# Attention over a 0/1 adjacency: more heads' sums from 0/1 patterns, and where the patterns are made

## The chip, the cores and the metric

The kernel runs on one core of a Trainium2 chip. The time is the device time of one execution in microseconds (us). TensorE (PE) multiplies matrices, VectorE (DVE), ScalarE (ACT) and GpSimd (POOL) work on vectors, SyncE (SP) only issues DMAs; ACT and POOL issue DMAs too.

## What is computed

Four graph layers follow one another on x (2708 x 512, float32) with one adjacency adj (2708 x 2708, 0/1, symmetric, with ones on its diagonal). Each is x + layer(relu(layernorm(x)), adj). Layers 0, 1 and 3 are a normalised sum, a mean of the first 64 neighbours and a mean of all neighbours, each with dense products. Layer 2 is the attention, which the change is about:

```python
Wh = jnp.einsum('nd,hdo->hno', x, W)              # 8 heads, 64 outputs each
f1 = jnp.einsum('hno,ho->hn', Wh, a1)
f2 = jnp.einsum('hno,ho->hn', Wh, a2)
e = jax.nn.leaky_relu(f1[:, :, None] + f2[:, None, :], negative_slope=0.2)
e = jnp.where(adj[None, :, :] > 0, e, NEG_INF)
attention = jax.nn.softmax(e, axis=-1)
h_prime = jnp.einsum('hnm,hmo->hno', attention, Wh)
out = jax.nn.elu(h_prime)
```

## The kernel before

**Tiles and steps.** The 2708 nodes lie in NC = 22 chunks of R = 126 rows (the last has 62). The attention works through units: u0 and u1 are head 0's output columns 0 to 1384 and 1384 to 2708, u2 to u7 the heads 1 to 6 whole, u8 and u9 head 7's two column parts. Each unit runs over the 22 chunks m of neighbours; a step is one pair of unit and chunk, 220 in all. In the step the kernel does this:

- `make` (L883, DVE) builds the weights t of the chunk, 126 rows by the unit's columns: max(row value, column value) times the 0/1 adjacency vT (uint8, kept in SBUF). The exponentials of leaky_relu factor into a row part `rb` and a column part `ec`, so that the maximum of the two is the weight. There are TILES = 4 buffers of t.
- `scale` (ACT) multiplies the chunk's rows of Wh by the factor `ef` into whs (L872), and, unless the step is "by side", a column of ones too (L874). There are 4 buffers of whs and 3 of wh, loaded by SP three chunks at a time.
- `multiply` (PE, in the helper at L1066) adds Wh-weighted rows into the accumulators av, in float32, and, unless by side, the weights' sums from t into the accumulators sums.
- A step *by side* gets its sums otherwise. `compare` (ACT, L901) turns t into a bf16 0/1 pattern b (2 buffers) by a very steep Sigmoid, which tells which of the two factors was the maximum; `multiply_sides` (PE, one step later) multiplies it by `parts`, three bf16 pieces that add up to each float32 factor. `by_side` holds for chunks with m % 5 in (1, 3, 4), 13 of 22, in the heads 1 to 6.

**Sums by side need a count.** The patterns give the sums over the neighbours on one side. The rest comes from the sum over all neighbours of the second factor: for each by-side chunk, `mask` (L1138, ACT) copies the chunk's adjacency as bf16 into four buffers of tag "x" (126 x 677 each), and `count_neighbors` (PE, L1150) multiplies it by `parts2`, the pieces for the heads, into two accumulators adj_sums; after the last one, eight copies (L1163) send them out. The masks are planned for the steps from 11 on, chunk i's count for step 13 + 2i: five counts stand in u0, eight in u1.

**split** (L1122 to L1127) makes the pieces: ACT casts a piece (L1122), DVE subtracts it (L1124), three rounds for each of two factors; the last ACT copy (L1127) fills parts2.

**Head changes.** The next head's row values are loaded by `load_row1` (SP, 126 copies of a row, 1332.8 KB, two buffers rb) and raised by `exp_row` (ACT, L847). Exp and Sigmoid need different function tables, so each exp_row in a by-side stretch brings two table loads. `evict` copies a finished unit's accumulators (ACT, L1105) and stores them.

**What sets the order.** The main loop hands out each step's operations in the order scale, make (three steps ahead), compare (one ahead), multiply, multiply_sides (one behind), then what `behind(s, fn, ...)` has put into `plan` for that step. A scheduler then orders each engine's queue by priority and estimated times, so that a planned step isn't a fixed place; `tc.issue_after(ins)` keeps an operation behind a named one. Buffers that are reused add waits. PE, ACT, DVE, POOL and SP each work through their own queue in order.

The layer-3 loads `load3` are planned for the last 16 steps and take "x" buffers (5). The rows a1 and a2 of the dense stage ahead (`arow`) have buffers of their own, and the bias row b3, which L1258 adds in layer 3, has one too.

Of the kernel before, what the change touches and what calls it, by code (L numbers as in the profile page):

```python
# [8 lines left out]
F32 = mybir.dt.float32  # L9
F32R = mybir.dt.float32r  # L10
BF16 = mybir.dt.bfloat16
# [3 lines left out]
AF = mybir.ActivationFunctionType  # L15
# [5 lines left out]
P = 128  # L21

R = 126
# [7 lines left out]
SLOPE2 = 0.2  # L31
# [13 lines left out]
def fast_layers(  # L45
# [36 lines left out]
    nc = tc.nc  # L82
    N, D = x_in.shape
    H, _, O = w2.shape
    NC = -(-N // R)
    NF = D // P
# [5 lines left out]
    def rows(c):  # L92
        return min(R, N - c * R)
# [17 lines left out]
    XBUFS = 5  # L111
# [8 lines left out]
    weights = ctx.enter_context(tc.tile_pool(name="weights", bufs=2))  # L120
    dram = ctx.enter_context(tc.tile_pool(name="dram", bufs=1, space=DRAM))

    common = ctx.enter_context(tc.tile_pool(name="common", bufs=2))

    ps = ctx.enter_context(tc.tile_pool(name="ps", bufs=8, space=PSUM, reuse_waits="tile"))
# [47 lines left out]
            nc.sync.dma_start(w[:, i], src[i * P : (i + 1) * P, :])  # L173
        return w

    def load_row(pool, src, name, tag=None):

        t = pool.tile([P, D], F32, name=name, tag=tag or name)
        nc.sync.dma_start(t, bass.AP(tensor=src.tensor, offset=src.offset, ap=[[0, P], [1, D]]))
        return t  # L180

# [165 lines left out]
    vT = []  # L347
# [69 lines left out]
    with ExitStack() as ring_ctx:  # L417
        ring = ring_ctx.enter_context(tc.tile_pool(name="ring", bufs=NC - 1, side="right"))
# [29 lines left out]
        with tc.tile_pool(name="l0", bufs=2) as wk:  # L448
            units = [(g, m) for g in range(len(groups)) for m in range(NC)]
            tiles, uppers, acc, sums, xs = {}, {}, {}, {}, {}  # L450
# [344 lines left out]
    BY_SIDE = [m for m in range(NC) if m % 5 in (1, 3, 4)]  # L795
# [6 lines left out]
    cut = EARLY * R // 8 * 8  # L802
    units = [(h, 0, N) for h in range(H)]
# [3 lines left out]
    steps = [(u, m) for u in range(len(units)) for m in range(NC)]  # L807

    def by_side(u, m):
        return 0 < units[u][0] < H - 1 and m in BY_SIDE  # L810

    whd = dram.tile([N, D], F32, name="whd")
    avT = dram.tile([D, N], F32, name="avT")
# [2 lines left out]
    sumT = dram.tile([NS, N], F32, name="sumT")  # L816
# [4 lines left out]
    at = at_ctx.enter_context(tc.tile_pool(name="att", bufs=1, reuse_waits="tile"))  # L821
# [3 lines left out]
    parts = at.tile([R, NC * H * 8 + S], BF16, name="parts")  # L825
    nc.gpsimd.memset(parts, 0.0)
    parts_of = parts[:, : NC * H * 8].rearrange("p (m h k) -> p m h k", h=H, k=8)
    parts2 = at.tile([R, NC, H, 3], BF16, name="parts2")
    nc.gpsimd.memset(parts2, 0.0)
    one6 = at.tile([R, S], F32, name="one6")  # L830
    nc.gpsimd.memset(one6, 0.0)
    nc.gpsimd.memset(one6[:, 6:7], 1.0)
    row, weight, wh, whs, acc, sides, made = {}, {}, {}, {}, {}, {}, []

    def load_row1(h, lo, hi):

# [7 lines left out]

    def exp_row(h, lo, hi):
        t = row[h][:, lo:hi]
        nc.scalar.activation(t, t, AF.Exp, scale=1.0 - SLOPE2)  # L847


    GROUP = 3  # L850
# [15 lines left out]
    def scale(s):  # L866

        u, m = steps[s]
        h, q = units[u][0], rows(m)
        t = at.tile([R, O + S], F32, name="whs", bufs=4)  # L870
        by = ef[:q, m, h : h + 1]
        nc.scalar.activation(t[:q, :O], wh.pop((u, m))[:q], AF.Copy, scale=by)  # L872
        if not by_side(u, m):
            nc.scalar.activation(t[:q, O:], one6[:q], AF.Copy, scale=by)  # L874
        whs[s] = t

    def make(s):
        u, m = steps[s]
        h, lo, hi = units[u]
        q = rows(m)  # L880
        g, k = where[m]
        t = at.tile([R, N], F32, name="t2", bufs=TILES)
        ins = nc.vector.scalar_tensor_tensor(  # L883
            t[:q, : hi - lo],
            row[h][:q, lo:hi],
            ec[:q, m, h : h + 1],
            vT[g][:q, k, lo:hi],
            op0=ALU.max,
            op1=ALU.mult,
        )  # L890
        weight[s] = t
        made.append(ins.ins)
# [16 lines left out]

    l2p = ctx.enter_context(ExitStack())  # L910
    pp = l2p.enter_context(tc.tile_pool(name="l2p", bufs=2, side="right", reuse_waits="tile"))
    ar = [load_row(pp, a, f"arow{i}") for i, a in enumerate((a1, a2))]

    products, firsts = {}, {}

# [73 lines left out]
    e3_ctx = ctx.enter_context(ExitStack())  # L989
    e3 = e3_ctx.enter_context(tc.tile_pool(name="e3", bufs=2, side="right", reuse_waits="tile"))  # L990
    er = e3.tile([R, NC, H], F32, name="er", bufs=1)
    rest = e3.tile([R, NC, H], F32, name="rest", bufs=1)
    kept3, l3_weights = {}, []


# [56 lines left out]
    def pieces(w):  # L1052

        k = -(-w // 512)
        cuts = [round(i * w / k) for i in range(k + 1)]
        return list(zip(cuts, cuts[1:]))

    def sizes_of(u):
        _, lo, hi = units[u]
        return (hi - lo) // 2, (hi - lo) // 4  # L1060
# [38 lines left out]
    def evict(u, which):  # L1099
        h, lo, hi = units[u]  # L1100
        size = sizes_of(u)[which]
        dst, height, step = (sumT, 7, S) if which else (avT, O, O)
        for p, (a, b) in zip(acc[u][which], pieces(size)):
            t = common.tile([P, D], F32, name="out", tag="t", bufs=3)
            nc.scalar.copy(t[:, : b - a], p[:, : b - a])  # L1105
            for j in range(P // step):
                nc.sync.dma_start(
                    dst[h * height : (h + 1) * height, lo + j * size + a : lo + j * size + b],
                    t[j * step : j * step + height, : b - a],
                )  # L1110

    def split():

        nc.scalar.mul(eb, ec, -STEEP * ABOVE)
        for i in range(2):
            e = ef
            if i:
                nc.vector.tensor_tensor(rest, ec, ef, ALU.mult)
                e = rest
            for k in range(3):  # L1120
                part = parts_of[:, :, :, 3 * i + k]
                nc.scalar.copy(part, e)  # L1122
                if k < 2:
                    nc.vector.tensor_tensor(rest, e, part, ALU.subtract)  # L1124
                    e = rest
        heads = slice(1, H - 1)
        nc.scalar.copy(parts2[:, :, heads], parts_of[:, :, heads, 3:6])  # L1127


    quarter = N // 4  # L1130
    counted, masks = [], {}

    def mask(i, j):
        m = BY_SIDE[i]
        q = rows(m)
        g, k = where[m]
        t = masks[i, j] = common.tile([P, D], F32, name="x", bufs=XBUFS).bitcast(BF16)
        nc.scalar.copy(t[:q, :quarter], vT[g][:q, k, j * quarter : (j + 1) * quarter])  # L1138

    def count_neighbors(i):  # L1140
        m = BY_SIDE[i]
        q = rows(m)
        if i == 0:
            counted.extend(
                ps.tile([P, 512], F32, name="adj_sums", tag="ps") for _ in pieces(quarter)
            )
        w = parts2[:q, m].rearrange("p h k -> p (h k)")
        for p, (a, b) in zip(counted, pieces(quarter)):
            for j in range(4):
                nc.tensor.matmul(  # L1150
                    p[j * S : j * S + 3 * H, : b - a],
                    w,
                    masks[i, j][:q, a:b],
                    start=(i == 0),
                    stop=(i == len(BY_SIDE) - 1),
                )
        if i < len(BY_SIDE) - 1:
            return
        for p, (a, b) in zip(counted, pieces(quarter)):
            t = common.tile([P, D], F32, name="out", tag="t", bufs=3)  # L1160
            for j in range(4):
                own = slice(j * S, j * S + 3 * H)
                nc.scalar.copy(t[own, : b - a], p[own, : b - a])  # L1163
                nc.sync.dma_start(
                    sumT[7 * H :, j * quarter + a : j * quarter + b], t[own, : b - a]
                )

    def exp_nodes():
# [10 lines left out]
    def behind(s, fn, *args):  # L1179
        plan.setdefault(s, []).append((fn, args))  # L1180
# [3 lines left out]
    behind(4, exps2, slice(EARLY, NC))  # L1184
    behind(5, load_row1, *units[1])
    behind(6, exp_row, *units[1])
    behind(9, split)
    behind(30, load_l3_weights)
    behind(30, exp_nodes)
    for u in range(2, len(units)):  # L1190
        if units[u][1] == 0:
            s = max(1, u - 1) * NC
            behind(s + 4, load_row1, units[u][0], 0, N)
            behind(s + 8, exp_row, units[u][0], 0, N)
    for u in range(len(units)):
        behind((u + 1) * NC - 1, evict, u, 0)
        behind(min((u + 1) * NC, len(steps) - 1), evict, u, 1)
    for i in range(len(BY_SIDE)):
        for j in range(4):
            behind(11 + 2 * i + j // 2, mask, i, j)  # L1200
        behind(13 + 2 * i, count_neighbors, i)

    for at_step, fn, c in (
        (16, load3, 0),
# [33 lines left out]

    with ExitStack() as stack:
        ring = stack.enter_context(tc.tile_pool(name="ring3", bufs=NC - 1, reuse_waits="tile"))  # L1240
        b3 = e3.tile([P, D], F32, name="b3", bufs=1)
        nc.sync.dma_start(
            b3, bass.AP(tensor=bias3.tensor, offset=bias3.offset, ap=[[0, P], [1, D]])
        )
# [688 lines left out]
def kernel(tc: tile.TileContext, *args: bass.AP):  # L1933

    nc = tc.nc
    with tc.tile_pool(name="verdict", bufs=1) as pool:
        verdict = pool.tile([1, 1], I32, name="verdict")
        fast_layers(tc, *args, verdict)
        odd = nc.values_load(verdict[0:1, 0:1], min_val=0, max_val=P + 1)
        with tc.If(odd > 0):  # L1940
            general_layers(tc, *args)
# [32 lines left out]
```

## Time and profile before

| what | us |
|---|---|
| median of three runs (1822.24 to 1826.04) | 1825.34 |
| the profiled execution | 1825.62 |
| its span | 1823.8 |
| attention, first to last matmul of L1066 | 856.6 to 1417.1 |
| PE's first matmul of u0, u1, u2 | 856.6, 898.6, 938.3 |
| PE's first matmul of u3, u4, u5, u6, u7 | 1002.4, 1073.8, 1138.5, 1203.4, 1268.3 |
| PE's first matmul of u8, u9 | 1334.9, 1374.1 |
| DVE's first make of u0, u1, u2 | 833.5, 892.8, 933.3 |
| DVE's first make of u7, u8, u9 | 1261.0, 1327.6, 1368.9 |
| L1138, a mask copy of 126 x 677 on ACT, 48 of them (and 4 of 62 rows) | 0.76 |
| L1105, a copy of an accumulator on ACT | 0.43 to 0.53 |

A line of groups names the source line, the engine, the operation, output and inputs with their shapes, how many there were, their busy time and the mean in ns of one; after the last bar stands how long the engine sat idle just before them, and what it then waited for. A line of waits adds these up by waiter and releaser. A table of stretches gives, for each stretch of the span, its length and the busy time of each engine. Matmuls overlap one another, so the time from one's start to the next one's is shorter than the mean of one.

### The profile page before, as it was taken

Reading aid. Unit: us, or ns where it says so; the run is one execution under the profiler, and the core shown is the slowest. Engines: PE = TensorE matmul, PEld = TensorE weight load, DVE = VectorE, ACT = ScalarE, POOL = GpSimd, SP = SyncE. Lnnn points to the kernel's source line nnn. Section 1 sums busy time; section 2 is a strip of 40 time slices with the busy share of each in tenths; the row PEclk is TensorE's granted clock in tenths of the full one; section 3 lists DMA queues with packets and bytes.
Section 4 is the critical chain, followed back from the end, with each engine's and each line's share of the span. In section 5 each row is a group of like instructions: output and inputs, shape, how many; then the busy total and the mean of one; then the engine's idle time right before and its main releaser. Section 6 shows DMA issues by size and latency. Waiting matters only on the chain.

```text
span 1823.8 us, 30715 instructions
## 1 busy us (share of the span) xinstructions
PE 1785.4 (98%) x11884; PEld 1041.1 (57%) x11884; DVE 1308.3 (72%) x1836; ACT 796.6 (44%) x1542; POOL 245.2 (13%) x241
## 2 busy tenths in 40 slices
PE   9999999999999999999999999999999999999998
PEld 4456777654448887644544344334444445488776
DVE  4942998855446655788999999999989777533334
ACT  2632777731210000156896676776744566400000
POOL 0101323301110211266000000000000222100000
PEclk9999999999999999999999999999999999999999
DMA  7632666635462211353231121121012444313221
GB/s 247 193 112 67 204 209 199 193 80 115 116 143 58 71 57 46 94 149 104 73 89 35 33 61 41 29 61 53 15 36 53 130 139 131 95 34 109 82 68 45
DMA packets 165553, 176.62 MB, mean 97 GB/s; under 512 B 94830, under 2 KB 115792, under 8 KB 164516
## 3 DMA queue, kind: packets, MB, share of 16 engines
q1 hardware_dynamic: 143170, 131.47, 26.3%
q10 hardware_dynamic: 18484, 33.28, 5.3%
q0 software_dynamic: 3744, 9.82, 1.6%
q8 instruction: 95, 1.56, 0.4%
q14 instruction: 60, 0.49, 0.1%
HBM read 111.35 MB, written 55.15 MB: 91 GB/s over the span
## 4 chain that ended last, share of the span: by engine, by line
PE 77%; DVE 11%; DMA 5%; issue 4%; POOL 1%; ACT 1%; SPq 0%; ACTq 0%; DVEq 0%; POOLq 0%
PE acc L368 32%; PE av L1066 16%; PE nb_ps L184 6%; PE sums L1066 6%; DVE t L883 5%; PE self_ps L184 4%; PE wh_ps L184 3%; PE line_ps L184 2%; PE h_ps L184 2%; DVE cum L494 2%; PE fused_ps L312 2%; PE hT_ps L212 1%; DMA x<-x 1%; DMA rb<-rT 1%; DMA packed<-two 1%
## 5 line engine op out<-in xcount | busy, mean ns | idle before, releaser
L883 DVE SCALAR_TENSOR_TENSOR t<-rb,ec,vT 126x2708 f32<-126x2708 f32 (+2 forms) x220 | 532.4, 2469 | 20.6 <-PE sums L1066 10.9
L368 PE MATMUL acc<-halves,kt 126*126 126x512 f32 x1848 | 435.5, 395 | 3.7 <-DVE kt L741 2.1
L1066 PE MATMUL av<-t,whs 126*32 126x451 f32 (+3 forms) x4576 | 436.5, 515 | 0.6 <-DVE ln_mv L191 0.6
L368 PEld LDWEIGHTS acc<-halves,kt 126*126 126x126 f32 x1848 | 342.6, 186 | 93.1 <-DVE kt L741 6.5
L1066 PEld LDWEIGHTS av<-t,whs 126*32 126x32 f32 (+1 forms) x4576 | 160.2, 110 | 206.9 <-issue 181.7
L368 PE MATMUL acc<-halves,ar 126*126 126x512 f32 x924 | 235.4, 408 | 4.3 <-ACT ar L488 2.4
L901 ACT ACTIVATE b<-t,eb 126x2708 bf16<-126x2708 f32 (+1 forms) x78 | 199.0, 2551 | 21.2 <-DVE t L883 21.0
L368 PEld LDWEIGHTS acc<-halves,ar 126*126 126x126 f32 x924 | 171.0, 189 | 55.4 <-issue 8.1
L193 ACT ACTIVATE ln_rs<-ln_mv,eps 126x1 f32<-126x1 f32 x88 | 25.6, 293 | 341.1 <-DMA x<-x 199.2
L741 DVE SCALAR_TENSOR_TENSOR kt<-lastr,index,vT 126x504 fp32r<-126x504 int16 (+3 forms) x154 | 110.4, 728 | 80.9 <-PE acc L368 80.7
L1291 DVE CAST kt<-vT 126x504 fp32r<-126x504 uint8 (+3 forms) x154 | 55.9, 365 | 138.2 <-PE acc L368 138.2
L1066 PE MATMUL sums<-t,whs 126*32 126x338 f32 (+5 forms) x1568 | 140.5, 451 | 5.1 <-ACT out L1105 5.1
L872 ACT ACTIVATE whs<-wh,ef 126x64 f32<-126x64 f32 x220 | 76.6, 350 | 130.1 <-PE sums L1066 73.7
L1033 POOL TENSOR_SCALAR z<-y 126x512 f32<-126x512 f32 x22 | 44.0, 2000 | 664.8 <-DVE y L1026 656.0
L494 DVE TENSOR_TENSOR_SCAN cum<-ai,deg 126x504 int16<-126x504 int32 (+2 forms) x110 | 128.4, 1180 | 0.6 <-DMA ai<-in_adj 0.6
L522 ACT ACTIVATE cum<-cum,limit 126x504 int16<-126x504 int16 (+3 forms) x132 | 88.1, 667 | 59.9 <-DVE deg L502 58.9
L1066 PEld LDWEIGHTS sums<-t,whs 126*32 126x32 f32 (+1 forms) x1568 | 55.3, 109 | 73.1 <-issue 40.7
L189 DVE BATCH_NORM_STATS2 ln_st<-x 126x6 f32<-126x512 f32 x88 | 60.2, 685 | 45.7 <-DMA x<-x 30.8
L184 PE MATMUL h_ps<-w0s,hT 128*126 128x512 f32 x176 | 81.2, 605 | 4.7 <-ACT hT L214 3.5
L184 PE MATMUL nb_ps<-wfn,hT 128*126 128x512 f32 x176 | 80.7, 602 | 3.1 <-ACT hT L214 3.1
L184 PE MATMUL wh_ps<-w2s,hT 128*126 128x512 f32 (+1 forms) x176 | 79.4, 593 | 0.0
L184 PE MATMUL nb_ps<-wn,hT 128*126 128x512 f32 x176 | 79.2, 592 | 0.0
(182 smaller groups left out, 1870.6 us busy)
## 6 DMA issues: line engine op xcount, KB each, us to landing
x<-x SPq DMA_DIRECT2D x105, 252.0 KB
x<-x ACTq DMA_DIRECT2D x84, 252.0 KB
ai<-in_adj SPq DMA_DIRECT2D x84, 249.0 KB
x<-in_x SPq DMA_DIRECT2D x42, 252.0 KB
rb<-rT SPq DMA_DIRECT2D x7, 1332.8 KB
wh<-whd SPq DMA_DIRECT2D x70, 94.5 KB
packed<-two POOLq DMA_DIRECT2D x44, 124.5 KB, 4.5
whd<-wh SPq DMA_DIRECT2D x21, 252.0 KB
```

The lines of the kernel that those rows point to most:

```text
L184: nc.tensor.matmul(po[:n], lhsT[:, f, :n], w[:, f, :], start=(f == 0), stop=(f == NF - 1))
L189: nc.vector.bn_stats(st[:n], xc[:n])
L368: nc.tensor.matmul(acc[:R], weight[:, k * R : (k + 1) * R], parts[:, i, :], start=(m == 0 and i == 0), stop=(m == NC - 1),)
L494: nc.vector.tensor_tensor_scan(cum[:n, :gw], ai[:n, :gw], ai[:n, :gw], 0.0 if g == 0 else deg[:n, m : m + 1], op0=ALU.add, op1=ALU.max,)
L522: nc.scalar.activation(cum[:n, :gw], cum[:n, :gw], AF.Sign, bias=limit[:n], scale=-1.0, accum_out=signs[:n, m, g : g + 1],)
L741: nc.vector.scalar_tensor_tensor(by_chunk(kt, cs), lastr[:, cs[0] * R : (cs[-1] + 1) * R].rearrange("p (c r) -> p c r", r=R), index[:R, m ...
L872: nc.scalar.activation(t[:q, :O], wh.pop((u, m))[:q], AF.Copy, scale=by)
L883: ins = nc.vector.scalar_tensor_tensor(t[:q, : hi - lo], row[h][:q, lo:hi], ec[:q, m, h : h + 1], vT[g][:q, k, lo:hi], op0=ALU.max, op1=AL ...
L901: nc.scalar.activation(b[:q, : hi - lo], weight[s][:q, : hi - lo], AF.Sigmoid, bias=eb[:q, m, h : h + 1], scale=STEEP,)
L1033: nc.gpsimd.tensor_scalar(z, y, 0.0, None, op0=ALU.min)
L1066: nc.tensor.matmul(p[j * S : (j + 1) * S, : b - a], lhsT, rhs[:, part * size + a : part * size + b], start=(s % NC == 0), stop=(s % NC == ...
L1291: nc.vector.tensor_copy(by_chunk(kt, cs), pattern(m, cs))
```

## The change

- `by_side` holds for u1 to u8: the second part of head 0 and the first part of head 7 are by side too.
- `parts2` covers the 13 by-side chunks only, in two versions by column half: the left half for the heads 1 to 7, the right half for the heads 0 to 6. Six small ACT copies fill it instead of one.
- `mask` is one DMA a chunk, issued by POOL, that reads 126 x 2708 uint8 from vT and writes bf16 into one of the two buffers b of the patterns, instead of four ACT copies into "x" buffers. It is planned for step 6 + i, and the count for step 10 + i. Twelve counts then stand in u0 in the built order, the thirteenth in u1's first step. The counts' column quarters are cut at [0, 692, 1384, 2046, 2708], so that pieces have 346 or 331 columns. In POOL's queue the first two mask DMAs stand ahead of the dense stage's first product, the other eleven each behind a wait on PE, for the count that frees the buffer.
- `load_row1` is planned two steps after the head's start (before: four) and `exp_row` nine (before: eight), and exp_row is kept behind the last scale handed out until then.
- Buffers: the a1 and a2 rows go into a weight buffer ("w"), `rest` into a "t" buffer, the av copies of full heads into "x" buffers, b3 into the ring of layer 3.

```diff
     def by_side(u, m):
-        return 0 < units[u][0] < H - 1 and m in BY_SIDE
+        return 0 < u < len(units) - 1 and m in BY_SIDE
...
-    parts2 = at.tile([R, NC, H, 3], BF16, name="parts2")
+    parts2 = at.tile([R, len(BY_SIDE), 2, H, 3], BF16, name="parts2")
...
     def exp_row(h, lo, hi):
         t = row[h][:, lo:hi]
-        nc.scalar.activation(t, t, AF.Exp, scale=1.0 - SLOPE2)
+        with tc.issue_after(scaled[-1]) if scaled else ExitStack():
+            nc.scalar.activation(t, t, AF.Exp, scale=1.0 - SLOPE2)
...
-    ar = [load_row(pp, a, f"arow{i}") for i, a in enumerate((a1, a2))]
+    arows = weights.tile([P, NF, D], F32, name="arows", tag="w")
+    ar = [load_row(None, a, None, into=arows[:, i]) for i, a in enumerate((a1, a2))]
...
-            t = common.tile([P, D], F32, name="out", tag="t", bufs=3)
+            tag, bufs = ("x", XBUFS) if (lo, hi) == (0, N) and which == 0 else ("t", 3)
+            t = common.tile([P, D], F32, name="out", tag=tag, bufs=bufs)
...
-        heads = slice(1, H - 1)
-        nc.scalar.copy(parts2[:, :, heads], parts_of[:, :, heads, 3:6])
-    quarter = N // 4
+        for i, heads in enumerate((slice(1, H), slice(0, H - 1))):
+            for r in sorted({m % 5 for m in BY_SIDE}):
+                ms = [m for m in BY_SIDE if m % 5 == r]
+                src = parts_of[:, r :: 5, heads, 3:6]
+                at_i = [BY_SIDE.index(m) for m in ms]
+                nc.scalar.copy(parts2[:, at_i[0] : at_i[-1] + 1 : 3, i, heads], src)
+    fourths = [0, cut // 2, cut, (cut + N) // 2, N]
...
-    def mask(i, j):
+    def mask(i):
...
-        t = masks[i, j] = common.tile([P, D], F32, name="x", bufs=XBUFS).bitcast(BF16)
-        nc.scalar.copy(t[:q, :quarter], vT[g][:q, k, j * quarter : (j + 1) * quarter])
+        t = masks[i] = at.tile([R, N], BF16, name="b", bufs=2)
+        nc.gpsimd.dma_start(t[:q], vT[g][:q, k, :N])
...
-            behind(s + 4, load_row1, units[u][0], 0, N)
-            behind(s + 8, exp_row, units[u][0], 0, N)
+            behind(s + 2, load_row1, units[u][0], 0, N)
+            behind(s + 9, exp_row, units[u][0], 0, N)
...
-        for j in range(4):
-            behind(11 + 2 * i + j // 2, mask, i, j)
-        behind(13 + 2 * i, count_neighbors, i)
+        behind(6 + i, mask, i)
+        behind(10 + i, count_neighbors, i)
...
-        b3 = e3.tile([P, D], F32, name="b3", bufs=1)
+        b3 = ring.tile([P, D], F32, name="b3", bufs=1)
```

More of the change, by code (lines that the diff above doesn't have):

```diff
@@ L174, in load_weight, with load_row @@
         return w
-    def load_row(pool, src, name, tag=None):
-        t = pool.tile([P, D], F32, name=name, tag=tag or name)
+    def load_row(pool, src, name, into=None):
+        t = into
+        if t is None:
+            t = pool.tile([P, D], F32, name=name)
         nc.sync.dma_start(t, bass.AP(tensor=src.tensor, offset=src.offset, ap=[[0, P], [1, D]]))
@@ L832, in fast_layers @@
     nc.gpsimd.memset(one6[:, 6:7], 1.0)
-    row, weight, wh, whs, acc, sides, made = {}, {}, {}, {}, {}, {}, []
+    row, weight, wh, whs, acc, sides, made, scaled = {}, {}, {}, {}, {}, {}, [], []
     def load_row1(h, lo, hi):
@@ L871, in scale @@
         by = ef[:q, m, h : h + 1]
-        nc.scalar.activation(t[:q, :O], wh.pop((u, m))[:q], AF.Copy, scale=by)
+        ins = nc.scalar.activation(t[:q, :O], wh.pop((u, m))[:q], AF.Copy, scale=by)
         if not by_side(u, m):
@@ L875, in scale @@
         whs[s] = t
+        scaled.append(ins.ins)
     def make(s):
@@ L991, in fast_layers @@
     er = e3.tile([R, NC, H], F32, name="er", bufs=1)
-    rest = e3.tile([R, NC, H], F32, name="rest", bufs=1)
     kept3, l3_weights = {}, []
@@ L1114, in split @@
         nc.scalar.mul(eb, ec, -STEEP * ABOVE)
+        rest = common.tile([P, D], F32, name="rest", tag="t", bufs=3)
+        rest = rest[:R, : NC * H].rearrange("p (m h) -> p m h", h=H)
         for i in range(2):
@@ L1125, in split, with pieces_of @@
                     e = rest
-        heads = slice(1, H - 1)
-        nc.scalar.copy(parts2[:, :, heads], parts_of[:, :, heads, 3:6])
-    quarter = N // 4
+        for i, heads in enumerate((slice(1, H), slice(0, H - 1))):
[5 more added lines that the diff above has]
+    fourths = [0, cut // 2, cut, (cut + N) // 2, N]
     counted, masks = [], {}
-    def mask(i, j):
+    def pieces_of(j):
+        return pieces(fourths[j + 1] - fourths[j])
+    def mask(i):
         m = BY_SIDE[i]
@@ L1144, in count_neighbors @@
             counted.extend(
-                ps.tile([P, 512], F32, name="adj_sums", tag="ps") for _ in pieces(quarter)
+                ps.tile([P, 512], F32, name="adj_sums", tag="ps") for _ in pieces_of(0)
             )
-        w = parts2[:q, m].rearrange("p h k -> p (h k)")
-        for p, (a, b) in zip(counted, pieces(quarter)):
+        for n, p in enumerate(counted):
             for j in range(4):
+                a, b = pieces_of(j)[n]
                 nc.tensor.matmul(
                     p[j * S : j * S + 3 * H, : b - a],
-                    w,
-                    masks[i, j][:q, a:b],
+                    parts2[:q, i, j // 2].rearrange("p h k -> p (h k)"),
+                    masks[i][:q, fourths[j] + a : fourths[j] + b],
                     start=(i == 0),
@@ L1158, in count_neighbors @@
             return
-        for p, (a, b) in zip(counted, pieces(quarter)):
+        for n, p in enumerate(counted):
             t = common.tile([P, D], F32, name="out", tag="t", bufs=3)
             for j in range(4):
+                a, b = pieces_of(j)[n]
                 own = slice(j * S, j * S + 3 * H)
@@ L1164, in count_neighbors @@
                 nc.sync.dma_start(
-                    sumT[7 * H :, j * quarter + a : j * quarter + b], t[own, : b - a]
+                    sumT[7 * H :, fourths[j] + a : fourths[j] + b], t[own, : b - a]
                 )
```

## The prediction

> **What bounds the kernel now.** I read the page's chain first, then the busy time of each engine by stretch of the attention, then the groups inside a stretch, then TensorE's waits. The chain gives the attention's matmuls (L1066) some 22% of the span and VectorE's weights (L883) 5%:
>
> ```profile
> PE 77%; DVE 11%; DMA 5%; issue 4%; POOL 1%; ACT 1%; SPq 0%; ACTq 0%; DVEq 0%; POOLq 0%
> ```
>
> The change touches only the attention, 856.6 to 1417.1 us. By unit (head 0's two parts; heads 1 to 6; head 7's two parts) the busy times are:
>
> ```profile
> core 0: us, PE busy (x) PEld busy (x) DVE busy (x) ACT busy (x) POOL busy (x), PEclk, DMA share, GB/s
> 856.60:898.60 42.00, 42.00 (x574) 20.65 (x577) 38.75 (x34) 31.08 (x78) 2.50 (x2) 1.00 0.34 100
> 898.60:938.30 39.70, 39.70 (x603) 18.38 (x596) 35.22 (x21) 35.79 (x87) 0.00 (x0) 1.00 0.29 78
> 938.30:1334.90 396.60, 391.50 (x4653) 165.34 (x4649) 389.78 (x134) 286.83 (x312) 0.00 (x0) 0.99 0.16 43
> 1334.90:1374.10 39.20, 39.20 (x540) 17.06 (x536) 36.31 (x22) 14.38 (x49) 0.00 (x0) 1.00 0.16 37
> ```
>
> The two parts of head 0 and the first of head 7 are TensorE-bound: PE is busy for the whole stretch and DVE is not. The six full heads are different. Their makes:
>
> ```profile
> L883 DVE SCALAR_TENSOR_TENSOR t<-rb,ec,vT 126x2708 f32<-126x2708 f32 x125 | 369.7, 3031 | 4.4 <-PE sums L1066 2.1 <-PE av L1066 1.8 <-ACT b L901 0.5
> L901 ACT ACTIVATE b<-t,eb 126x2708 bf16<-126x2708 f32 x72 | 183.7, 2551 | 19.4 <-DVE t L883 19.1
> L847 ACT ACTIVATE rb<-rb 126x2708 f32<-126x2708 f32 x6 | 14.8, 2462 | 8.9 <-DMA rb<-rT 8.9
> L901 ACT ACT_TABLE_LOAD x7 | 9.0, 1283 | 0.1
> ```
>
> start every 2.951 us, and 22 x 2.951 = 64.9 us is exactly the spacing of heads 1, 3, 4 and 5. TensorE's matmul starts give av 0.758 us a piece of 451 columns, f32 sums 0.57, bf16 sums 0.145: 9 x (3 x 0.758 + 2 x 0.57) + 13 x (3 x 0.758 + 2 x 0.145) = 64.1 us. DVE bounds by 0.8 us a head. PE's only waits on another engine's result in the heads are at two head changes, 3.4 us near 1004 and 1.7 us near 1270:
>
> ```profile
> PE sums L1066 <- ACT out L1105: 5.1, 2, 3.4
> ```
>
> There ScalarE sat on exp_row (L847), waiting for the row's DMA ("8.9" in its row), and the copies that free TensorE's accumulators stood behind it.
>
> **What the Trainium skill says.** "DMA: Bandwidth & Descriptors", Anatomy of one DMA — SWDGE (gpsimd) path, gives about 2.0 us plus bytes/436e3. The trace is slower: packed<-two (124.5 KB) lands in 2.4 us at best, 4.5 in the median when other DMAs run; fused<-wf (1024 KB) in 5.1 where the formula says 4.4. That is 2.4 us + 346 KB per us above 124.5 KB. The same page, SWDGE vs HWDGE vs iDMA, says that a cast during a DMA goes through GpSimd's path only; no DMA of the program before casts, so the speed of a cast is not shown. "ScalarE: Activation LUTs", What ACT_TABLE_LOAD costs, gives 280 ns + 0.833 ns an element with a bias column: 2.54 us at 2708, trace 2551 ns; 1.38 us at 1324 and 1.43 at 1384, shapes that are not in the trace. Its 1283 ns table load is the trace's.
>
> **The change, part by part.**
>
> *(1) Part 0, plain work.* PE takes 42.06 us from first matmul to first matmul, with 5 counts in it at 0.3 us (L1150: two bf16 groups of 0.145). In the built order it now holds 12 counts, one a step from step 10: 42.06 + 7 x 0.3 = 44.2. The mask copies on ScalarE go (52 x 0.76 us), but ScalarE bounded nothing here: worth 0.
>
> *(2) Part 0, wait for parts2.* Count 0 moves from step 13 (882.8) into the middle of step 10, where PE stands at about 876.6. It needs parts2, which needs the last piece of split: DVE's rest operations stand at 870.3, 872.4, 874.3, 876.2 and 878.2, each about two us after the other behind ScalarE's casts (L1122 1.0 us each), the last cast ends at 879.7, and now six small copies follow (about 0.3 us each; before, one of 0.53): 881.5. New stall 881.5 - 876.6 = 4.9 us. Behind it in PE's queue stand all av matmuls; DVE fills its four t buffers, which it already leads by, so it cannot bank the time. Bounds: 3 (copies overlap) to 6.
>
> *(3) Part 0, wait for the masks.* 13 casting DMAs write 126 x 2708 bf16 = 682 KB each into two buffers. The first two are issued before the attention, while GpSimd idles for 10 us ahead of its first product; the other 11 each stand on GpSimd behind the count two earlier, with nothing but later masks behind them. A step with a count lasts 2.04 us, so two last 4.08; count i+2 comes in time if issue to landing takes less than 4.08 - 0.3 - 0.3 (hand-overs) = about 3.5 us. By written bytes a mask takes 2.4 + (682 - 124.5)/346 = 4.0, by read bytes (341 KB) 3.0, and two are in flight together: I take 4.4-4.5. Stall 11/2 x (4.5 - 3.5) = 5.5 us; bounds 0 (read bytes count) to 21 (the cast halves the rate, below). Part 0 becomes 44.2 + 4.9 + 5.5 = 54.6, **+12.5**.
>
> *(4) Part 1 by side.* 13 of 22 steps replace an f32 sums group (0.56 us) by a bf16 one (0.145): 9 x 1.675 + 13 x 1.25 + one count 0.3 = 31.6, against 39.64. Makes: 22 x 1.504 = 33.1, of which DVE starts 5.8 early, so not the bound. ScalarE: 13 x 1.38 + 22 x 0.25 + 9 x 0.21 of scales (starts; 350 and 309 ns are its means) + 8 output copies of the counts 3.4 + out copies 1.3 + exp_row with two table loads 5.0 = 35, before 35.8 with casts. It is now near the bound. Two places bite: the copies after count 12 stand ahead of the next sigmoid (about 1 us), and the 5.4 us block of table load, exp_row, table load is covered by about two steps of lead, 3 us (2.4 us). 31.6 + 3.4 = 35.0, **-4.6**; bounds -7.5 and 0.
>
> *(5) Full heads.* exp_row now stands some ten scales into a head, where its DMA (6.6 us from issue to landing, issued at the head's start) has long landed; the row load itself is only planned two steps earlier on SP, and the buffer it waits for is free by then, so the wh loads behind it lose nothing. The head-change block goes; next late is DVE. DVE's own first make of head 1 to first make of head 7: 394.3 us now, 6 x 64.9 = 389.5 then: **-4.8**. PE gives up the lag it built (7.3 us behind DVE at head 7, 4.2 before the stall), which part 6 collects.
>
> *(6) Head 7, first part.* PE 9 x 1.746 + 13 x 1.31 + head change 0.8 = 33.5 (now 39.25); DVE 22 x 1.567 = 34.5 bounds. ScalarE: 13 x 1.43 + 7.4 + copies 2.7 = 29, below it. The second part stays PE-bound, 42.9.
>
> *(7) Costed at nothing.* Outputs into "x" buffers push layer 3's first x loads (252 KB) into head 7, tens of us ahead of use. b3 moves to the ring and is issued after the attention's last stores; it is needed about 5 us later by L1258, and lands with 1.5-2 us to spare (2 us if that is gone). The a rows in a weight buffer load earlier than before.
>
> **Sum**, along DVE, which bounds between. PE starts head 1 at 938.3 + 12.5 - 4.6 = 946.2, DVE 4.5 us ahead of it: 941.7 (now 933.3). + 389.5 + 34.5 = 1365.7 for DVE's start of the last part. PE follows by 2.2 us (a make of 1.66 and the hand-over): 1367.9, now 1374.1. **-6.2 us**. Around the span lie 1.8 us (1825.62 for 1823.8); the profiled run is 0.3 us above the median, 1825.34, so the forecast is 1819.1.
>
> **The rivals.**
>
> *A, the forecast*: masks a little late (issue to landing 3.9 to 5.2 us): 1816 to 1823, likeliest 1819.
>
> *B, masks in time*: they land by read bytes, in 3.5 us or less; stall 3 is 0 and the time 1813.5. For it: DMA traffic of part 0 falls to a few GB/s after 885. Against: 682 KB must be written every 2 us, 334 GB/s, about all that fused<-wf reached.
>
> *C, masks too slow, slower than before*: a casting DMA moves data at half the rate of a copy. Two in flight share it, so a mask costs 2 x 682/346 = 3.9 us where a step has 2.04: 11 x 1.9 = 21 us instead of 5.5, time 1834 (1826 to 1838). It decides from 2.04 + (5.5 + 6.2)/11 = 3.1 us per mask. For it: nothing in the trace shows a cast's rate, and 4.5 us was usual for a mere 124.5 KB; against: that was among 200 GB/s of other traffic.
>
> *D, ScalarE bounds part 1*: sigmoids, exp_row and copies run one behind the other with no overlap, 38-39 us, and the gain of part 1 is lost: 1823.7. For it: the sum in (4) is above PE's; against: b is double and DVE leads.
>
> That exp_row only moves its block into the head, so that PE stalls there, is the other half of D: 110 us of ScalarE's 397 in the heads are free, so unlikely.
>
> **Numbers.** A 0.48 (0.40 faster, 0.08 same), B 0.15 faster, C 0.22 (0.04 same, 0.18 slower), D 0.15 (0.02 faster, 0.10 same, 0.03 slower). Faster by over 0.2% (3.7 us, about what a measurement here can tell from none) 0.57, same 0.22, slower 0.21. Range 1811 (B with the parts2 wait at 3 us) to 1831, which leaves out about half of C.
>
> **What would show it.** Part 0 at 54-55 us of PE with two kinds of wait at the counts: one of 5 us for ScalarE's parts copy and about 11 of 0.5 us for mask DMAs; masks landing 4-5 us after issue. No PE wait on ScalarE's out copies at head changes; heads spaced 64.9. Part 1 near 35, head 7's first part near 34.5. Wrong if masks land in over 5.5 us, if PE waits on b (L901's new line) in part 1 for more than 5 us, or if a part 1 near 32 leaves it DVE-bound.

## The result, and the profile after

The change makes the kernel slower: 1833.16 us in the median (1830.17 to 1836.73, nine runs) against 1826.04 in the nine runs of before, ratio 1.0042 with a 95% interval of 1.003 to 1.0053. The forecast was 1819.1 in a range of 1811 to 1831. The profiled execution has a span of 1829.1 us (before 1823.8).

First the busy times by unit, cut at PE's first matmul of each unit, columns as in the prediction's table: head 0's two parts, the six full heads, head 7's first part.

```profile
857.30:916.40 59.10, 46.93 (x626) 20.03 (x629) 38.91 (x33) 20.47 (x66) 8.32 (x13) 1.00 0.82 200
916.40:953.30 36.90, 34.58 (x495) 17.76 (x495) 32.52 (x21) 35.36 (x59) 0.00 (x0) 1.00 0.25 63
953.30:1346.10 392.80, 389.62 (x4652) 160.99 (x4652) 391.06 (x134) 287.85 (x312) 0.00 (x0) 1.00 0.15 43
1346.10:1379.60 33.50, 33.50 (x488) 15.14 (x486) 32.99 (x21) 27.12 (x49) 0.00 (x0) 1.00 0.30 82
```

In the first part TensorE, which had been busy throughout, is now idle for 12 of 59 us, and the DMA engines' share has gone from 0.34 to 0.82. The second part is shorter, with ScalarE busy for 35.4 of its 36.9 us. From PE's first matmul of one unit to that of the next, and on to the end:

| stretch | before | after | difference | forecast |
|---|---|---|---|---|
| up to the attention | 856.58 | 857.32 | +0.7 | 0 |
| head 0, first part | 42.06 | 59.03 | +17.0 | +12.5 |
| head 0, second part | 39.64 | 36.90 | -2.7 | -4.6 |
| heads 1 to 6 | 396.61 | 392.87 | -3.7 | see below |
| head 7, first part | 39.25 | 33.44 | -5.8 | see below |
| head 7, second part, to the last av | 42.37 | 43.22 | +0.9 | 0 |
| rest of the span | 407.3 | 406.3 | -1.0 | 0 |

In the trace eleven counts start before the second part's first matmul and two after it, one fewer in the first part than in the built order.

What TensorE waited for in the attention, by waiter and releaser:

```profile
PE adj_sums L1168 <- DMA b<-vT: 11.0, 9, 2.3
PE sums L1072 <- ACT out L1113: 3.1, 1, 3.1
...
PE sums L1072 <- ACT b L907: 1.4, 1, 1.4
PE adj_sums L1168 <- ACT parts L1141: 1.3, 1, 1.3
```

The counts (L1168) waited nine times for mask DMAs; the wait for a pattern b, one of the prediction's signs of being wrong, stayed at 1.4 us. These are the answer on the DMA queues for 884 to 916 us of the same run, and the row of the mask DMAs in the page (KB of 1024 bytes each, 682 of the prediction's thousands; median us from issue to landing):

```profile
q0 software_dynamic: 1365, 6.50, 93.5%
...
b<-vT POOLq DMA_DIRECT2D x12, 666.4 KB, 6.0
```

In these 32 us the 16 DMA engines are full: 93.5% of their time is the masks' queue and 6.5% the other loads (a share is the sum of the packets' times, and can pass 100% in sum). 6.50 MB in 0.935 x 32 us are 217 GB/s, counted in bytes written. The median landing time of 6.0 us is above the 5.5 that the prediction named as a sign of being wrong. From the issue of the third mask to that of the last, 882.05 to 915.44, a mask takes 33.4/10 = 3.34 us where a step with its count has 2.04. The chain in order of time shows the same: from 882 to 916 us three quarters of it are these DMAs.

```profile
by line: DMA b<-vT 75.9%; PE adj_sums L1168 7.5%; PE av L1072 7.2%; PE sums L1072 5.5%; issue 3.9%; ACT out L1113 1.3%
```

In the full heads the makes have no idle time at all ahead of them, where 4.4 us stood before:

```profile
L889 DVE SCALAR_TENSOR_TENSOR t<-rb,ec,vT 126x2708 f32<-126x2708 f32 x125 | 369.2, 3028 | 0.0
```

### The profile page after: what moved, and what is told of

The parts are those of the page before. It is cut to its first block, busy times and chain, and to the rows that moved or that the text cites. A ratio compares the mean times of both kernels' runs of the same rounds, so it can differ in the third digit from the quotient of the medians.

```text
span 1829.1 us, 30470 instructions
## 1 busy us (share of the span) xinstructions
PE 1776.3 (97%) x11780; PEld 1031.5 (56%) x11780; DVE 1305.5 (71%) x1836; ACT 797.1 (44%) x1497; POOL 251.7 (14%) x254
## 4 chain that ended last, share of the span: by engine, by line
PE 82%; DVE 8%; DMA 6%; issue 2%; ACT 1%; POOL 1%; SPq 0%; DVEq 0%; ACTq 0%; POOLq 0%
PE acc L370 31%; PE av L1072 19%; PE nb_ps L186 8%; PE sums L1072 6%; PE self_ps L186 4%; PE line_ps L186 4%; PE wh_ps L186 2%; DVE cum L496 2%; PE h_ps L186 2%; DVE t L889 2%; PE fused_ps L314 2%; PE hT_ps L214 2%; DMA b<-vT 1%; DMA x<-x 1%; DMA ai<-in_adj 1%
## 5 line engine op out<-in xcount | busy, mean ns | idle before, releaser
L1072 PE MATMUL av<-t,whs 126*32 126x451 f32 (+3 forms) x4576 | 443.1, 514 | 1.4 <-DVE ln_mv L193 0.6
L907 ACT ACTIVATE b<-t,eb 126x2708 bf16<-126x2708 f32 (+4 forms) x104 | 236.1, 2270 | 41.9 <-DVE t L889 40.2
L370 PEld LDWEIGHTS acc<-halves,ar 126*126 126x126 f32 x924 | 169.1, 186 | 54.1 <-issue 7.7
L1072 PE MATMUL sums<-t,whs 126*32 126x338 f32 (+3 forms) x1360 | 130.0, 450 | 3.1 <-ACT out L1113 3.1
L191 DVE BATCH_NORM_STATS2 ln_st<-x 126x6 f32<-126x512 f32 x88 | 60.5, 687 | 50.9 <-DMA x<-x 36.9
L1072 PEld LDWEIGHTS sums<-t,whs 126*32 126x32 f32 x1360 | 50.9, 109 | 62.4 <-issue 34.2
```

The source lines that it names most:

```text
L191: nc.vector.bn_stats(st[:n], xc[:n])
L370: nc.tensor.matmul(acc[:R], weight[:, k * R : (k + 1) * R], parts[:, i, :], start=(m == 0 and i == 0), stop=(m == NC - 1),)
L907: nc.scalar.activation(b[:q, : hi - lo], weight[s][:q, : hi - lo], AF.Sigmoid, bias=eb[:q, m, h : h + 1], scale=STEEP,)
L1072: nc.tensor.matmul(p[j * S : (j + 1) * S, : b - a], lhsT, rhs[:, part * size + a : part * size + b], start=(s % NC == 0), stop=(s % NC == ...
```

## The experiments

The theory after reading the two traces: the masks' DMAs are bound by the DMA engines (bytes, not the cast and not the hand-over of buffers), and that alone turns a gain of some 10 us into a loss. Rivals: the cast halves the rate; a fixed time from issue to landing with two buffers sets the pace; the parts by side are worth little in themselves. The median of the runs of before beside the experiments lay between 1823.3 and 1824.9.

**1. No cast, the same bytes written.** Two rows of vT are read as bf16.

```diff
-        nc.gpsimd.dma_start(t[:q], vT[g][:q, k, :N])
+        at_k = min(k, sizes[g] - 2) * VW
+        src = vT[g].rearrange("p k v -> p (k v)")[:q, at_k : at_k + 2 * N]
+        nc.gpsimd.dma_start(t[:q], src.bitcast(BF16))
```

> The mask DMAs of the changed kernel read 682 KB of bf16 instead of 341 KB of uint8 and write the same 682 KB, so that nothing is cast; the counts are of other numbers, the instructions and their order are unchanged. If the cast itself is slow (half the rate of a copy, rival C of the prediction), masks then land in 4 to 4.5 us instead of 6.0, PE waits 3 to 6 us for them instead of 11, and the first part of head 0 takes some 52 us of PE instead of 59. If it is the written bytes beside the other traffic, masks stay at 6 us and the part at 58 to 60 us. If reads count too, masks take 7 us or more and the part gets longer.

Measured: landing in 6.0 us in the median (4.3 to 7.6), PE's wait for masks 11.6 us in eight waits, the part 61.2 us. TensorE's granted clock was 0.97 in this part, so that its length compares with the others to some 2 us only. The times to landing, and the queue's row for the 32 us from 890:

```profile
DMA to landing us min/median/max: 4.3/6.0/7.6
...
q0 software_dynamic: 1284, 6.08, 82.6%
```

That is 6.08 MB in 0.826 x 32 us, 230 GB/s, against 217 with the cast. So a mask made by a cast costs, within 6%, what a copy of the finished mask costs, and rival C's 3.9 us for a cast beside 2.0 for a copy does not hold. But the run takes the cast away and doubles the bytes read at once. That the written bytes decide, with a cast that is nearly free, would explain the result; a time set by the bytes read, with a cast at half the rate, would explain it too, and run 2 fits both. No run here separates the two. The whole time, 1840.09 us in one run, isn't used: in this run the attention began 5 us later, after stages that the edit doesn't touch.

**2. No cast, half the bytes written** (341 KB, as many as are read, in the change too).

```diff
-        nc.gpsimd.dma_start(t[:q], vT[g][:q, k, :N])
+        nc.gpsimd.dma_start(t[:q].bitcast(mybir.dt.uint8)[:, :N], vT[g][:q, k, :N])
...
-                    masks[i][:q, fourths[j] + a : fourths[j] + b],
+                    masks[i][:q, a:b],
```

> The mask DMAs copy 341 KB of uint8 uncast into the first half of the buffer, and the counts read that half for all quarters (other numbers, the same instructions). If transfer sets the stall (by bytes or by cast), masks land in 3 to 3.5 us, PE's wait for them falls to 0 to 2 us and the first part of head 0 to 47 to 49 us of PE, the whole to 1819 to 1823. If a fixed cost of a DMA and of its semaphores sets it, masks stay near 6 us and the part at 59.

Measured: landing in 3.4 us in the median; the part takes 48.9 us, the whole 1821.19 in one run. The times to landing, the queue's row for 884 to 906 us, and PE's waits:

```profile
DMA to landing us min/median/max: 2.5/3.4/5.4
...
q0 software_dynamic: 788, 3.35, 55.8%
```

```profile
PE adj_sums L1168 <- DMA b<-vT: 1.8, 3, 1.1
```

The engines are no longer full (3.35 MB in 0.558 x 22 us are 273 GB/s) and PE's wait is almost gone. A fixed time from issue to landing is thus not what sets the pace. Of the 17 us lost in the first part, this gives 10 back.

**3. Masks by ScalarE, head 0 not by side.** What is left of the change is head 7's first part, ScalarE's order and the buffers.

```diff
     def by_side(u, m):
-        return 0 < u < len(units) - 1 and m in BY_SIDE
+        return 1 < u < len(units) - 1 and m in BY_SIDE
...
+        lo, hi = fourths[j : j + 2]
+        t = masks[i, j] = common.tile([P, D], F32, name="x", bufs=XBUFS).bitcast(BF16)
+        nc.scalar.copy(t[:q, : hi - lo], vT[g][:q, k, lo:hi])
...
-        behind(6 + i, mask, i)
-        behind(10 + i, count_neighbors, i)
+        for j in range(4):
+            behind(11 + 2 * i + j // 2, mask, i, j)
+        behind(13 + 2 * i, count_neighbors, i)
```

> The changed kernel with the masks made by ScalarE again (four copies a chunk, counts every second step from 13 on, as before) and head 0 not by side; head 7's first part by side, ScalarE's order and the buffers as changed. If the mask DMAs and the early counts alone made the change slower, the first part of head 0 returns to 42 us and the second to 39.6, the heads keep DVE's spacing of 64.9 us, head 7's first part its 33.4 us: 1826.0 - 4 - 5.8 = 1816, ratio 0.994 to 0.9955. If the gains in the heads and in head 7 do not reach the end, 1822 to 1827.

Measured: 1815.53 us, ratio 0.9952 (0.9936 to 0.9969): faster than both kernels. The first part is back at 41.9 us and head 7's first part stays at 33.4. The second part takes 41.1 us, though, 1.5 more than before.

**4. ScalarE's order alone.** The kernel before with the change's edits of the order (scaled is the list of scales handed out, filled as in the change):

```diff
-            behind(s + 4, load_row1, units[u][0], 0, N)
-            behind(s + 8, exp_row, units[u][0], 0, N)
+            behind(s + 2, load_row1, units[u][0], 0, N)
+            behind(s + 9, exp_row, units[u][0], 0, N)
...
-        nc.scalar.activation(t, t, AF.Exp, scale=1.0 - SLOPE2)
+        with tc.issue_after(scaled[-1]) if scaled else ExitStack():
+            nc.scalar.activation(t, t, AF.Exp, scale=1.0 - SLOPE2)
```

> The kernel before with ScalarE's order alone: the row load two steps after a head's start, exp_row nine, kept behind the last scale. If DVE's makes and PE's matmuls both need 64.9 us a head, DVE's first make of head 1 to first make of head 7 goes from 394.3 to 389.5 us, PE's matmuls follow with at most one wait of 3 us left, and 3 to 5 us reach the end: 1821 to 1823, ratio 0.9975 to 0.9985. If PE's lag absorbs it, 1825 to 1826, ratio 1.

Measured: 1821.3 us, ratio 0.9983 (0.9976 to 0.9991). The heads go from 396.6 to 391.8 us of PE, and head 0's second part from 39.64 to 41.15. In that part one step takes 3.36 us: head 1's exp_row (914.8 to 917.3) now stands among the mask copies, and the next count waits for a mask.

```profile
PE adj_sums L1152 <- ACT x L1140: 0.9, 2, 0.6
```

Runs 3 and 4 differ by 0.31 points of ratio, 5.7 us. Head 7's first part, 5.8 us shorter in run 3, accounts for it, which leaves nothing for the buffers, the other difference of the two.

**5. Head 1's row as before.** Run 3, but head 1's row load and exp_row keep their old places, and exp_row is not kept behind a scale:

```diff
-            behind(s + 2, load_row1, units[u][0], 0, N)
-            behind(s + 9, exp_row, units[u][0], 0, N)
+            behind(s + (4 if u == 2 else 2), load_row1, units[u][0], 0, N)
+            behind(s + (8 if u == 2 else 9), exp_row, units[u][0], 0, N)
...
-        with tc.issue_after(scaled[-1]) if scaled else ExitStack():
+        with tc.issue_after(scaled[-1]) if h > 1 else ExitStack():
```

> The kernel of the third run (masks by ScalarE, head 7's first part by side, head 0 not) with head 1's row load and exp_row planned as before and not kept behind a scale. In the third and fourth run head 1's exp_row stood among ScalarE's mask copies in head 0's second part; one step there took 3.36 us instead of 1.97. If that is the cause of the second part's 41.1 us, it returns to 39.6 and the whole to 1814, ratio near 0.9945. If not, the part stays at 41 and the ratio at 0.995.

Measured: 1813.29 us, ratio 0.9943 (0.9923 to 0.9963), the fastest here; the step of 3.36 us is gone and the second part at 39.7:

```profile
855.70:897.90 42.20, 42.17 (x574) 20.59 (x577) 38.78 (x34) 31.76 (x83) 2.51 (x2) 1.00 0.40 118
897.90:937.60 39.70, 39.70 (x600) 21.56 (x591) 35.17 (x21) 35.80 (x87) 0.00 (x0) 1.00 0.24 67
937.60:1329.30 391.70, 389.31 (x4652) 166.14 (x4648) 389.51 (x134) 288.39 (x313) 0.00 (x0) 1.00 0.15 41
```

The interval overlaps that of run 3; that this edit is worth 1.4 us rests on the two profiles.

**6. Three buffers b in the changed kernel**, for masks and patterns:

```diff
-        t = masks[i] = at.tile([R, N], BF16, name="b", bufs=2)
+        t = masks[i] = at.tile([R, N], BF16, name="b", bufs=3)
```

> The changed kernel with three buffers b instead of two. If the DMA engines are full while masks move (theory: 3.3 us a mask whatever the number in flight), one more mask is ready ahead of time and the first part of head 0 gets shorter by 3 us, to 56; masks then take 8 to 9 us each from issue to landing, with three in flight. If the hand-over of buffers sets the pace (each mask waits for the count two earlier), the period falls to (6.0 + 0.6)/3 = 2.2 us and the part to 47 to 49.

Measured: landing in 8.7 us in the median with three in flight, the first part 57.4 us, the whole 1833.74 in one run. The times to landing, and the queue's row for 884 to 916 us:

```profile
DMA to landing us min/median/max: 5.1/8.7/10.0
...
q0 software_dynamic: 1366, 6.45, 97.3%
```

The bytes per us are the same as with two buffers; a third mask in flight only waits longer. The hand-over is not the cause.

**7. Masks by DMA, with time.** Run 5 with the change's mask DMAs; against the change, beside run 5's edits of by_side and of head 1:

```diff
-        behind(6 + i, mask, i)
-        behind(10 + i, count_neighbors, i)
+        behind(6 + 2 * i, mask, i)
+        behind(10 + 2 * i, count_neighbors, i)
```

> As the fifth run, but the masks come by DMA into the two buffers b, and the counts stand two steps apart from step 10, through the second part of head 0, which is not by side and so leaves b free. A mask then has about four steps, 7.6 us, from issue to need. If only the rate of the masks made them slow, PE waits for none of them: parts of 42 to 44 us (with a wait of 1 to 3 us for parts2 at the first count) and 39 to 40 us, the whole within 2 us of the fifth run. If DMA masks slow other work too (loads, the rows of the next head), 5 us more or above.

Measured: 1815.77 us, ratio 0.9954 (0.9938 to 0.9969), which run 5's interval overlaps. Masks still take 5.8 us to land, and PE waits for none of them:

```profile
PE adj_sums L1168 <- ACT parts L1141: 1.2, 1, 1.2
```

The parts take 44.5 and 39.5 us; in the first, the step with the first count is 1.7 us longer than others with a count, for parts2. So masks by DMA at this pace, one in 3.8 us, do no harm beyond this that the measurement can tell; one in 2 us does.

**8. Masks by ScalarE, head 0 by side.** Run 3 with the change's own condition:

```diff
-        return 1 < u < len(units) - 1 and m in BY_SIDE
+        return 0 < u < len(units) - 1 and m in BY_SIDE
```

> The changed kernel with ScalarE's masks, but with head 0's second part by side as in the change. ScalarE then has 31 mask copies, 13 sigmoids, the scales, exp_row and 13 copies to do in that part, some 57 us. If ScalarE bounds it, the part takes 50 us or more of PE instead of 36.9 and the whole is 1822 to 1830; if the two parts by side were worth what PE's count of groups says, it takes 34 and the whole 1810.

Measured: 1828.18 us in one run. Head 0's second part takes 54.4 us with ScalarE busy for 54.1:

```profile
896.10:950.50 54.40, 46.49 (x544) 21.80 (x534) 32.89 (x21) 54.11 (x87) 0.00 (x0) 0.94 0.13 33
```

With the masks in these places, head 0 by side thus cannot have ScalarE make them.

**9. Later counts in the changed kernel.**

```diff
-        behind(10 + i, count_neighbors, i)
+        behind(13 + i, count_neighbors, i)
```

> The changed kernel with every count three steps later (from step 13 on; masks planned as in the change, so that two are ready). The prediction added a wait for parts2 and waits for masks. If the eleven masks that must follow the first count, at 3.3 us each, are one chain, the wait for parts2 goes (3 us with what lies around it) but the chain only starts about 2 us later: the two parts of head 0 together take 95 to 98 us of PE, as in the change (95.9). If the two waits add up, they take 92 to 93.

Measured: 53.8 and 44.8 us, together 98.6 where the change has 95.9 (1830.49 us in one run).

```profile
PE adj_sums L1168 <- DMA b<-vT: 12.5, 10, 2.0
```

The wait for parts2 is gone and nothing is gained: from PE's first matmul of the attention, the third mask is issued after 27.0 us where the change has 24.7. That the two parts are longer still is not read: TensorE's granted clock was 0.93 in this run's second part.

**10. Almost without the two waits.** Runs 2 and 9 together, with head 1's row as in run 5.

> Counts from step 13 on, masks as uncast copies of 341 KB (the counts read the first half of the buffer for all quarters: other numbers, the same instructions), and head 1's exp_row as in the kernel before: what the change would be worth with neither wait. If the fifth run (head 0 not by side) is near the best of this form, because head 0's part by side is paid for by ScalarE's sigmoids and copies and by PE's order, the two parts take 79 to 82 us together (81.9 in the fifth run) and the whole 1812 to 1815, ratio 0.993 to 0.996. If part by side is worth what PE's groups say, 76 us or less and 1808.

Measured: 1820.24 us, ratio 0.9975 (0.9966 to 0.9984); 44.25 and 39.75 us for the two parts, 84.0 together, above what was expected.

```profile
PE av L1072 <- ACT whs L877: 3.6, 2, 2.4
...
PE adj_sums L1168 <- DMA b<-vT: 2.8, 3, 1.1
```

The wait for parts2 is gone; of the waits for masks, 2.8 us are left, and two new ones for ScalarE's scales take 3.6. So this form of the change stays behind run 5, whose parts take 81.9: in the second part PE is busy for only 34.1 of 39.7 us, and these waits use up what the bf16 sums save. The theory's first half stands, the second does not: with the masks nearly in time the change is worth 4.4 us, not 10, and the 10 of run 5 come with head 0 left as it was.

## Why the prediction was wrong

**The step that failed is (3), the wait for the masks.** The place and the mechanism were right, the size was not: 5.5 us forecast, about 13.4 measured. (From step 13, the first that waits for a mask, to the end of the part the change takes 32.3 us; the same nine steps of run 5 take 17.7, and 18.9 with the four counts that they lack.) The term that was mis-sized is the time from issue to landing, 4.4-4.5 us forecast, 6.0 measured; with it the formula gives 11/2 x (6.0 - 3.5) = 13.8. The 4.5 came from a line through two DMAs, packed<-two and fused<-wf, 346 KB per us, both from SBUF to memory and neither with another of its size behind it. Runs 1, 2 and 6 show that here the landing time is not a property of one DMA: what the 16 engines move sets it, 217 GB/s of written bytes with the cast and 230 without, and 682 KB then occupy all engines for 3.1 us, so that two masks in flight each take twice that. Why these copies within SBUF run at this rate, and what share the cast has in it, stays open.

The rate also gives the threshold: 3.34 us a mask is above the 3.1 at which the prediction said the change turns slower. Rival C thus named the right place and the right sign. Its 3.9 us a mask and its 21 us of stall were too much, and that its 1834 came so near the measured 1833.16 is luck: the waits that it had too long made up for what steps (4) and (5) had too short.

**Step (2) was wrong in two ways.** The last copy into parts2 ended at 881.6 us, forecast 881.5. But PE reached count 0 only at 879.6, since ten matmuls of step 11 stand ahead of it, and started it at 880.9, behind the first of the six copies; its wait was 1.3 us, and the two steps with the first two counts took 1.7 us more than such steps do without a wait (5.8 against 4.1), not 4.9. And it is not a term to be added: in run 9 it is gone, the chain of masks starts later, and the two parts get no shorter.

**Step (4), second part of head 0**: 36.9 us, forecast 35.0. ScalarE was full: 13 sigmoids at 1.39 us (forecast 1.38), exp_row, three table loads and eight copies fill the part. The forecast had two table loads; the first sigmoid needs one of its own. Both places named did bite: PE waited 0.6 us for a scale behind the eight copies and 1.4 us for a pattern behind exp_row.

```profile
L907 ACT ACTIVATE b<-t,eb 126x1324 bf16<-126x1324 f32 x12 | 16.7, 1389 | 0.0
...
L907 ACT ACT_TABLE_LOAD x2 | 2.6, 1283 | 0.7 <-issue 0.7
L852 ACT ACTIVATE rb<-rb 126x2708 f32<-126x2708 f32 x1 | 2.5, 2464 | 0.0
...
L852 ACT ACT_TABLE_LOAD x1 | 1.3, 1283 | 0.0
```

So rival D's mechanism was there in part; with the masks nearly in time (run 2) the part still took 35.9.

**Step (5), the full heads, was right for DVE and wrong for PE.** DVE's first make of head 1 to first make of head 7 took 389.4 us, forecast 389.5. But PE did not "give up the lag it built": 3.2 us behind DVE at head 1, it is 6.6 behind at head 7. Two things were wrong. The prediction's 64.1 us a head left out the head change, for which step (6) does count 0.8 us. In runs 1 to 5, 9 and 10, where PE starts head 3 some 7.5 us behind DVE, its heads follow every 64.7 us and DVE's every 64.9: PE catches up 0.2 us a head, not 0.8. And it comes no nearer than 6.6 us. At the changes to heads 2 to 6 the copies that free its accumulators stand on ScalarE behind a sigmoid that waits for DVE's second make, and PE's first f32 sums of the head start 0.05 us after the first of these copies ends. Only at head 2, where PE came 3.5 us behind DVE, is this long enough to show as a wait of PE, 3.1 us. The later ones, 0.2 us each, are seen only among the waits of its weight loads (PEld), whose sum has head 2's 3.9 us in it:

```profile
PEld sums L1072 <- ACT out L1113: 8.7, 11, 3.9
```

**Step (6), head 7's first part**: 33.44 us, forecast 33.5 from PE's groups and 34.5 from DVE's. PE came in late and bounds it; DVE's 37.25 us include its waits for buffers. Run 4, where this part takes 39.25, confirms the size.

**Step (7)** held: no wait for b3 or for x loads shows in the profile after.

The sum thus missed by 11.7 us at the last part's start (1379.6 against 1367.9): 4.5 in head 0's first part, where step (3) was 7.9 too low and step (2) 3.2 too high, 1.9 in its second, 0.7 ahead of the attention, and the rest, 4.6, from PE's lag, which the sum had assumed to shrink. So step (3) is the largest miss, but not the whole: with 13.4 us in it the forecast would have been 1827, no gain and still below what was measured. The profiled run, 1830.97 us, lies another 2.2 below the median. What stays open is whether masks in smaller pieces, with buffers of their own, could serve head 0 by side in time; it wasn't tried. Run 10 leaves little room for it.

## What to carry to other kernels

Before a copy is moved from an engine to a DMA, divide its bytes by the time between two of its uses and compare with what the DMA engines move in DMAs of the same kind that follow one another, not with the landing time of a lone one: here 682 KB every 2.04 us were asked of engines that moved 217 GB/s. A second in-flight buffer hides latency, but not a full queue; more time between the uses does (run 7). And when a stall is removed between two engines, check that the one behind has spare time before counting on it to catch up: here it had 0.2 us in 64.9.

## What the runs showed of the hardware

A DMA within SBUF that converts 341 KB of uint8 to 682 KB of bf16 ran at 217 GB/s of written bytes with all 16 engines full (the changed kernel, 884 to 916 us). One that copies 682 KB of bf16 ran at 230 (run 1), one that copies 341 KB at 273 (run 2). So making the 2-byte mask by a cast took about as long as copying it; how much of that is the cast and how much the bytes, these runs don't show. With three such DMAs in flight instead of two, each took 8.7 us instead of 6.0 (run 6), and the bytes moved in 32 us stayed the same, 6.45 MB against 6.50.
